# Moving accumulators between PSUM banks, loads into spare buffers, and the last norms in pairs, in a two-layer graph-attention kernel

## The chip, the cores and the metric

The kernel runs on one core of a Trainium2 chip. The metric is the device time of one execution in microseconds. The core has five engines that run their own instruction streams and meet at semaphores: TensorE (PE, matrix products; its weight loads are shown apart as PEld), VectorE (DVE), ScalarE (ACT), GpSimd (POOL) and SyncE (SP), which here only issues loads and stores. Matrix products land in PSUM, which has eight banks; a tile of 128 partitions by 512 float32 values fills one bank.

## The reference

There are 4096 nodes with 512 features, and one dense 0/1 adjacency matrix `adj` (4096 x 4096, symmetric, with ones on the diagonal). Two layers follow each other, each with a residual and a normalisation over the 512 features.

```python
def layer0(X, A, W, a_self, a_neigh, b):          # 8 heads of 64
    feats = einsum('nf,hfo->hno', X, W)
    dense = (feats . a_self)[:, :, None] + (feats . a_neigh)[:, None, :]
    dense = where(dense > 0, dense, 0.2 * dense) * A
    out = einsum('hij,hjo->hio', softmax(dense, -1), feats) + b
    return relu(out as (4096, 512))

def layer1(x, b, edge, ptr, Wq, bq, Wk, bk, Wv, bv):   # 32 graphs of 128 nodes
    mask = same graph
    a = where(mask, (x Wq' + bq) (x Wk' + bk)' / sqrt(512), 0)
    scores = (a + b + edge) * where(mask, 1, -1e6)
    return (softmax(scores) * mask) @ (x Wv' + bv)

x = layernorm(x + layer0(x, adj, ...))
x = layernorm(x + layer1(x, adj, adj, ...))
```

Layer 0 is a sum over all 4096 neighbours of each node. In layer 1 only the diagonal blocks of 128 by 128 count.

## The kernel before

**Layer 0.** The scores of a head depend on a node and on its neighbour only through one number each, so that the exponential of a score is the larger of two products. The kernel uses that: for a tile of 128 neighbours and 1024 nodes, one DVE instruction makes `q = max(p_row, d) * at` (L1560), with `p_row` a row of numbers of the nodes, `d` a column of the neighbours and `at` the adjacency tile. PE then adds three kinds of sums over the neighbours:

- `accf` (L1584): features `f_s` times `at`, two matmuls of weights for each tile and half;
- `acc` (L1607): features `g_s` times `q`, eight matmuls of 32 columns for each tile;
- `dens` (L1623): columns of exponentials `e_b` times `mark`, where `mark` tells which of the two products was larger (L1570 on ACT, one of eight at L1565 on DVE). In pass 0 there is also `ae` (L1499).

The work goes in four passes `r` over pairs of heads, each in four chunks `c` of 1024 nodes, each over 32 neighbour tiles `j`. A cycle takes eight `j` in passes 0 to 2 (`wide=8`), four in pass 3. PE's order in a cycle is: accf, then half of the bringing of later adjacency tiles, acc, dens, ae, and the other half of the bringing. In pass 0 bringing means eight transposes on PE (L614, `turned_steps`) into a PSUM bank, two casts on ACT (L625, `cast_steps`) into two `at` tiles, and a store of each to `at_d`; later passes load `at` from there. Some tiles are "folded": they take another formula (L1548, L1551, L1555), and their sums go to accf alone.

A setup makes the features of all nodes first. Its last part overlaps the first cycle: the transposes L773 give the last rows of exponentials, and `columns_of_last` turns them back into columns: four transposes L791 into a bank of `misc`, and the copy L794 into `pu_all`. `misc` deals out single PSUM banks in turn, for everything that is read back soon.

**PSUM.** The setup holds `ps_setup` (three banks) and `ps_feat` (four banks, the features). When they close, `ps_acc_f` takes five banks (`dens` one, `acc` two, `accf` two) from the place where ps_setup began, and the next pool takes the `ae` bank and, in pass 0, a second bank for `misc`. After pass 0, `misc` turns over three banks. A pool that takes the place of a closed one waits for the closed one's last readers.

**Layer 1** runs in blocks of four row tiles (512 nodes), interleaved with pass 3, in pieces that are dealt out by plan strings (`run_plan`); the last blocks run after pass 3. For each block, `rows_of_layer_0` loads the input `x1b` (L1257) and the heads of layer 0 from memory into `hp_l` (L1259, 384 columns, two buffers), adds them with a relu (L1264, the last 128 columns from `hst`, a tile in the chip's memory) and normalises them (`layernorm`: sums at L517 and L518 on DVE, the power on POOL at L520 and L521, the scaling at L525 on DVE, returned as a function that the plan calls at "F"). `layer_1` transposes them (L1085), forms the scores (L1105, L1132), and for each row tile the values (L1180, the bias L1189 into `v_t`, two buffers) and the outputs (L1196, L1198, a second `layernorm`, and the store L1206). In the last block the values of the last row tile are split: three of four matmuls before the outputs of the third, and the fourth after.

**What sets the order.** PE's instructions stand in program order. On the other engines a scheduler orders instructions as their inputs are due, except those that are pinned (`tc.keep_in_program_order`, `in_order`). SP's queue carries all loads in one line, so that a load that waits for its buffer holds the loads behind it.

Of the kernel before, what the change touches and what calls it, by code (L numbers as in the profile page):

```python
# [19 lines left out]
P = 128  # L20
# [384 lines left out]
def adjacency_streamed_path(  # L405
# [531 lines left out]
        columns_of_exponentials(NB - 1, misc([P, 4, 2 * H]))  # L937

    ckp = ctx.enter_context(tc.tile_pool(name="ck", bufs=2))
    psa = ctx.enter_context(tc.tile_pool(name="ps_acc_f", bufs=1, space=PSUM))  # L940
    dens = psa.tile([P, HB], F32, name="dens")
    nc.vector.memset(dens, 0.0)
# [62 lines left out]
    L1 = {}  # L1005
# [73 lines left out]
    def layer_1(blk, x1b, lp, lp1, lp2):  # L1079

        x1T = lp2.tile([P, FC, 4 * P], F32, name="x1T")
        for u in range(4):
            pt = misc([P, FC, P])
            for c in range(FC):
                nc.tensor.transpose(pt[:, c, :], x1b[:, u, ts(c, P)], ident)  # L1085
            nc.scalar.copy(x1T[:, :, ts(u, P)], pt)  # L1086
            if u == 1:
                yield
        a4 = lp.tile([P, 4, P], F32, name="a4")
        nc.sync.dma_start(  # L1090
            a4,
            bass.AP(
                tensor=adj.tensor,
                offset=adj.offset + 4 * blk * P * (N + 1),
                ap=[[N, P], [P * (N + 1), 4], [1, P]],
            ),
        )
        off = small.tile([P, 4], F32, name="off")
        rr = small.tile([P, 4], F32, name="rr")
        yield  # L1100
        zT = lp1.tile([P, FC, 4 * P], F32, name="zT")
        for c in range(FC):
            pz = misc([P, 4 * P])
            for f in range(FC):
                nc.tensor.matmul(  # L1105
                    pz,
                    L1["M"][:, f, ts(c, P)],
                    x1T[:, f, :],
                    start=(f == 0),
                    stop=(f == FC - 1),  # L1110
                )
            nc.scalar.activation(zT[:, c, :], pz, AF.Identity, bias=L1["zb"][:, c : c + 1])
            if c == 1:
                for u in range(4):
                    nc.scalar.activation(
                        a4[:, u, :], a4[:, u, :], AF.Copy, scale=2.0, accum_out=off[:, u : u + 1]
                    )
                    xu = lp.tile([P, F], F32, name="y_f")
                    nc.vector.tensor_tensor_reduce(
                        xu, x1b[:, u, :], L1["ub"], 1.0, 0.0, OP.mult, OP.add, rr[:, u : u + 1]  # L1120
                    )
                nc.gpsimd.tensor_scalar(off, off, 0.5, -float(P), op0=OP.mult, op1=OP.add)
                nc.gpsimd.tensor_add(off, off, n0[:, 4 * blk : 4 * blk + 4])
                nc.gpsimd.tensor_scalar(rr, rr, L1["cb"], None, op0=OP.add)
            if c % 2:
                yield
        pq = misc([P, 4, P])
        ns = a4
        nm = small.tile([P, 4], F32, name="nm_f")
        for u in range(4):  # L1130
            for f in range(FC):
                nc.tensor.matmul(  # L1132
                    pq[:, u, :],
                    zT[:, f, ts(u, P)],
                    x1T[:, f, ts(u, P)],
                    start=(u == 0 and f == 0),
                    stop=(f == FC - 1),
                    skip_group_check=True,
                )
        for u in range(4):  # L1140
            nc.vector.tensor_tensor_reduce(
                ns[:, u, :],
                pq[:, u, :],
                a4[:, u, :],
                -1.0,
                -LOWEST,
                OP.add,
                OP.min,
                nm[:, u : u + 1],
            )  # L1150
        nc.gpsimd.tensor_sub(nm, nm, rr)
        nc.gpsimd.tensor_scalar(nm, nm, 0.0, None, op0=OP.min)
        eb = small.tile([P, 4], F32, name="eb")
        nc.gpsimd.tensor_add(eb, nm, rr)
        den = small.tile([P, 4], F32, name="den_f")
        for u in range(4):
            nc.scalar.activation(
                ns[:, u, :],
                ns[:, u, :],
                AF.Exp,  # L1160
                bias=eb[:, u : u + 1],
                scale=-1.0,
                accum_out=den[:, u : u + 1],
            )
        e0 = small.tile([P, 4], F32, name="e0")
        nc.scalar.activation(e0, nm, AF.Exp)
        nc.gpsimd.tensor_tensor(e0, e0, off, OP.mult)
        nc.gpsimd.tensor_add(e0, e0, den)
        rd = small.tile([P, 4], F32, name="rd_f")
        nc.vector.reciprocal(rd, e0)  # L1170
        yield
        vs = {}

        def values(u, split=FC, pv=None):
            if pv is None:
                pv, fs = misc([P, F]), range(split)
            else:
                fs = range(split, FC)
            for f in fs:
                nc.tensor.matmul(  # L1180
                    pv,
                    x1T[:, f, ts(u, P)],
                    L1["wvT"][:, f, :],
                    start=(f == 0),
                    stop=(f == FC - 1),
                )
            if fs[-1] == FC - 1:
                vs[u] = lp.tile([P, F], F32, name="v_t")
                nc.vector.tensor_add(vs[u], pv, L1["bv"])  # L1189
            return pv  # L1190

        def rows_out(us):
            ys = []
            for u in us:
                po = misc([P, F])
                nc.tensor.matmul(po, pT[:, u, :], vs[u], start=True, stop=True)  # L1196
                y = lp.tile([P, F], F32, name="y_f")
                nc.vector.scalar_tensor_tensor(  # L1198
                    y, po, rd[:, u : u + 1], x1b[:, u, :], op0=OP.mult, op1=OP.add
                )  # L1200
                ys.append(y)
            layernorm(ys)()
            for i, u in enumerate(us):

                queue = nc.sync if blk >= NT // 4 - 2 else nc.gpsimd
                queue.dma_start(out[ts(4 * blk + u, P), :], ys[i])  # L1206

        values(0)
        pp = misc([P, 4, P])
        for u in range(4):  # L1210
            nc.tensor.transpose(pp[:, u, :], ns[:, u, :], ident)  # L1211
        pT = a4
        nc.scalar.copy(pT, pp)
        values(1)
        yield
        rows_out((0, 1))
        yield
        values(2)
        if blk == NT // 4 - 1:
            last = values(3, 3)  # L1220
            rows_out((2,))
            values(3, 3, last)
            yield
            rows_out((3,))
        else:
            values(3)
            yield
            rows_out((2, 3))
        yield
# [23 lines left out]
    def rows_of_layer_0(blk, hst, lp):  # L1253
        x1b = lp.tile([P, 4, F], F32, name="x1b")
        for u in range(4):
            it = 4 * blk + u
            nc.sync.dma_start(x1b[:, u, :], x[ts(it, P), :])  # L1257
            hp = lp.tile([P, F - FP], F32, name="hp_l")
            nc.sync.dma_start(hp, hs_d[ts(it, P), :])  # L1259
            for dst, src in (  # L1260
                (x1b[:, u, : F - FP], hp),
                (x1b[:, u, F - FP :], hst[:, it % CT, :]),
            ):
                nc.vector.scalar_tensor_tensor(dst, src, 0.0, dst, op0=OP.max, op1=OP.add)  # L1264
        plan["F"] = layernorm([x1b[:, u, :] for u in range(4)])
        return x1b

    def sums_to_rows(r, c, acc, accf, ae, u_row, later_by):
# [178 lines left out]
    def main_pass(r, ae=None, wide=4):  # L1447
# [9 lines left out]
        for c in range(NCH):  # L1457
# [46 lines left out]
                            stop=(j >= NT - 2),  # L1504
                        )

            acc = psa.tile([P, 2, HB], F32, name="acc")
            accf = psa.tile([P, 2, HB], F32, name="accf")
            marks = {}
            for j0 in range(0, NT, wide):  # L1510
# [70 lines left out]
                for j in cycle:  # L1581
                    for w in range(0 if folded(j) else 2):
                        for s in range(2):
# [4 lines left out]
                                start=(j == 0 and w == 0),  # L1588
                                stop=(j == NT - 1 and w == 1),
                            )  # L1590
                if at_step == 0:
                    columns_of_last()
                if r == 0 and (c, j0 + wide) == (NCH - 1, NT):

                    sums_over_a(c, cycle)
# [6 lines left out]
                for j in cycle:  # L1602
                    dst = accf if folded(j) else acc
                    for s in range(2):
                        for o in range(0, FP, 32):
# [6 lines left out]
                                stop=(j == NT - 1),  # L1612
                                skip_group_check=folded(j),
                            )
                if r == 0:
                    pieces(c, j0 // 4, 1)

# [36 lines left out]
    with tc.tile_pool(name="ps_ae", bufs=1, space=PSUM) as psx:  # L1654
        ae = psx.tile([P, HB], F32, name="ae")
        nc.vector.memset(ae, 0.0)
        banks.append(psx)
        main_pass(0, ae, wide=8)
        banks.remove(psx)
    first_pass.close()  # L1660
    banks.extend([ctx.enter_context(tc.tile_pool(name="ps_misc2", bufs=2, space=PSUM))] * 2)
    with tc.tile_pool(name="wl1", bufs=1, side="right") as wp:
        pools["wl1"] = wp
        work.append(weights_of_layer_1(keep, wp))
# [70 lines left out]
```

## Time and profile before

| what | us |
|---|---|
| median of three runs (2026.96 to 2030.07) | 2030.03 |
| the profiled execution | 2029.65 |
| its span | 2027.9 |
| PE busy | 1999.2 (99% of the span) |
| DVE busy | 1756.0 (87%) |
| ACT busy | 1524.7 (75%) |
| POOL busy | 231.2 (11%) |

The mean clock that PE was granted is 0.996 of full speed. The 40 slices of the span show PE at nine tenths or more in all but the last, which has seven tenths.

In the views below, a line of the timeline gives the start in us, the time from the first to the last of the merged instructions, the engine, the line of the code, the operation with the tile that it writes and those that it reads, the size, and how many were merged; in brackets stands the idle time of the engine before it and what ended that. A line of the waits gives who waited for whom, the total, the number of waits and the longest.

### The profile page before, as it was taken

The numbers are of one execution on the slowest core, as the hardware profiler recorded it, in microseconds if no ns is written. First come the engines' busy times: TensorE is split into PE (matmuls) and PEld (weight loads), VectorE is DVE, ScalarE is ACT, GpSimd is POOL, SyncE is SP. The second block draws the span as 40 slices with busy tenths as digits, with TensorE's granted clock in tenths as the row PEclk, the third lists the DMA queues.
The fourth block names the chain that finished last, engine by engine and source line by source line (L and its number), as shares of the span: only waits on it lengthen the run. The fifth ranks groups of instructions, "written<-read, shape, count | busy, mean of one in ns | idle before, by whom it ended". The sixth has DMA issues, their size and how long they took to land. (4 is left out here: it accounts for less than half of the span.)

```text
span 2027.9 us, 38096 instructions
## 1 busy us (share of the span) xinstructions
PE 1999.2 (99%) x14961; PEld 1023.0 (50%) x14961; DVE 1756.0 (87%) x2212; ACT 1524.7 (75%) x1872; POOL 231.2 (11%) x362
## 2 busy tenths in 40 slices
PE   9999999999999999999999999999999999999997
PEld 8884454545444444445445444444444444445443
DVE  5668999999999999898999999999997897899754
ACT  3348888888879898889889899999786666567420
POOL 1222222222200000000000000000020210211111
PEclk9999999999999999999999999999999999999998
DMA  6999999999999999799999899989976775775211
GB/s 210 248 328 270 296 283 277 287 292 295 323 368 342 364 343 327 257 340 310 317 318 333 304 347 334 333 280 366 320 255 197 243 246 163 233 278 161 73 55 44
DMA packets 209673, 555.74 MB, mean 274 GB/s; under 512 B 25068, under 2 KB 66412, under 8 KB 209484
## 3 DMA queue, kind: packets, MB, share of 16 engines
q1 hardware_dynamic: 145132, 430.64, 60.9%
q0 software_dynamic: 62272, 122.04, 23.4%
q8 instruction: 120, 1.97, 0.4%
q10 hardware_dynamic: 2080, 0.52, 0.1%
q14 instruction: 69, 0.57, 0.1%
HBM read 496.11 MB, written 107.35 MB: 298 GB/s over the span
## 5 line engine op out<-in xcount | busy, mean ns | idle before, releaser
L1560 DVE SCALAR_TENSOR_TENSOR q<-p_row,d_all,at 128x1024 f32<-128x1024 f32 x952 | 1154.9, 1277 | 94.2 <-PE acc L1607 38.4
L1570 ACT ACTIVATE mark<-q,nb_all 128x1024 fp8e4<-128x1024 f32 x824 | 907.6, 1148 | 137.9 <-DVE q L1560 126.9
L1607 PE MATMUL acc<-q,g_s 128*32 128x512 f32 x7616 | 841.9, 593 | 1.2 <-DVE q L1560 0.4
L1607 PEld LDWEIGHTS acc<-q,g_s 128*32 128x32 f32 x7616 | 248.5, 110 | 556.3 <-issue 495.5
L1584 PE MATMUL accf<-at,f_s 128*128 128x512 f32 x1904 | 464.3, 399 | 2.8 <-ACT at L625 2.7
L1584 PEld LDWEIGHTS accf<-at,f_s 128*128 128x128 f32 x1904 | 351.4, 189 | 109.2 <-issue 26.3
L1248 ACT ACTIVATE ck<-ck,neg_half_f 128x1024 f32<-128x1024 f32 x128 | 146.0, 1140 | 26.0 <-DMA ck<-in_adj_dram 25.7
L1249 ACT ACTIVATE ck<-ck,neg_quarter 128x1024 f32<-128x1024 f32 x128 | 146.4, 1144 | 1.9
L1555 ACT ACTIVATE mark<-q,below 128x1024 fp8e4<-128x1024 f32 x72 | 81.6, 1145 | 78.4 <-DVE q L1551 77.9
L1623 PE MATMUL dens<-mark,e_b 128*6 128x512 fp8e4 x2048 | 125.9, 379 | 1.8 <-DVE mark L1565 1.6
L807 PE MATMUL ps_fe<-w_sb_f,xT_f 128*128 128x264 f32 (+1 forms) x512 | 121.7, 395 | 1.0 <-ACT xT_f L727 1.0
L625 ACT CAST at<-ps_m 128x1024 fp32r<-128x1024 fp8e4 x124 | 117.2, 1026 | 0.0
L1180 PE MATMUL ps_m<-wvT,x1T 128*128 128x512 f32 x256 | 114.4, 594 | 0.0
L1105 PE MATMUL ps_m<-x1T,M_sb 128*128 128x512 f32 x256 | 113.0, 595 | 0.3 <-ACT x1T L1086 0.3
L807 PEld LDWEIGHTS ps_fe<-w_sb_f,xT_f 128*128 128x128 f32 x512 | 100.6, 200 | 15.7 <-ACT xT_f L727 1.8
L1371 POOL DMA_DIRECT2D hs_d<-hst x12 | 10.7, 896 | 827.6 <-DVE hst L1361 814.5
L626 POOL DMA_DIRECT2D at_d<-at x128 | 71.0, 555 | 269.9 <-ACT at L625 141.8
L1565 DVE TENSOR_SCALAR mark<-q,d_all 128x1024 fp8e4<-128x1024 f32 x128 | 95.9, 749 | 5.0 <-PE accf L1584 0.5
L1623 PEld LDWEIGHTS <-e_b 128*6 128x6 bf16 x2048 | 55.8, 86 | 79.3 <-issue 37.1
L1551 DVE SCALAR_TENSOR_TENSOR q<-q,c_all,at 128x1024 f32<-128x1024 f32 x72 | 90.5, 1274 | 0.0
L1105 PEld LDWEIGHTS ps_m<-x1T,M_sb 128*128 128x128 f32 x256 | 47.9, 190 | 59.6 <-issue 57.8
L1180 PEld LDWEIGHTS ps_m<-wvT,x1T 128*128 128x128 f32 x256 | 47.6, 190 | 56.4 <-issue 55.2
(209 smaller groups left out, 1315.3 us busy)
## 6 DMA issues: line engine op xcount, KB each, us to landing
at<-at_d SPq DMA_DIRECT2D x384, 512.0 KB, 6.0
at_d<-at POOLq DMA_DIRECT2D x128, 512.0 KB, 17.4
ck<-in_adj_dram SPq DMA_DIRECT2D x128, 512.0 KB, 5.5
f_s<-f_d SPq DMA_DIRECT2D x107, 512.0 KB, 7.5
g_s<-g_d SPq DMA_DIRECT2D x128, 256.0 KB, 5.8
f_d<-fst POOLq DMA_DIRECT2D x16, 1024.0 KB, 7.9
a_b<-in_adj_dram POOLq DMA_DIRECT2D x32, 512.0 KB, 21.1
p_row<-pu_d SPq DMA_DIRECT2D x32, 512.0 KB, 6.7
```

Source lines behind the costliest of these rows:

```text
L625: ends_of_setup["ACT"] = nc.scalar.copy(at, both[:, :, k])
L807: nc.tensor.matmul(pf[:, q, :, cols], tile_j(xTs[k][:, c].rearrange("p u n -> p (u n)"), u), w_sb[:, c, 4 * q : 4 * q + 4, cols], start=(c ...
L1105: nc.tensor.matmul(pz, L1["M"][:, f, ts(c, P)], x1T[:, f, :], start=(f == 0), stop=(f == FC - 1),)
L1180: nc.tensor.matmul(pv, x1T[:, f, ts(u, P)], L1["wvT"][:, f, :], start=(f == 0), stop=(f == FC - 1),)
L1248: tc.keep_in_program_order(nc.scalar.activation(ck, ck, AF.Square, bias=neg_half))
L1249: nc.scalar.activation(ck, ck, AF.Abs, bias=neg_quarter, accum_out=binp[:, k : k + 1])
L1560: ends_of_setup["Q"] = nc.vector.scalar_tensor_tensor(q, p_row[h], d_j, ats[r, c, j].bitcast(F32), op0=OP.max, op1=OP.mult)
L1565: nc.vector.tensor_scalar(mark, q, d_j, None, op0=OP.is_gt, saturate=False)
L1570: nc.scalar.activation(mark, q, AF.Sigmoid, bias=nb_all[:, j, hh : hh + 1], scale=BIG, saturate=False,)
L1584: nc.tensor.matmul(accf[:, s, :], f_s[j // 4][:, j % 4, w, :], ats[r, c, j][:, ts(s, HB)], start=(j == 0 and w == 0), stop=(j == NT - 1 an ...
L1607: nc.tensor.matmul(dst[o : o + 32, s, :], g_s[j // 4][:, j % 4, h, o % FH : o % FH + 32], qs[j, h][:, ts(s, HB)], start=(j == 0), stop=(j ...
L1623: nc.tensor.matmul(dens[lo : lo + 6, :], e_b[:, j, 2 * r + h, :], marks[j, h][:, ts(s, HB)], start=(j == 0), stop=(j == NT - 1),)
```

## The change

- **PSUM pools.** `acc` gets a pool of its own (`ps_acc_q`, two banks) and the second bank of `misc` another (`ps_misc1`); these two open first and so take the three banks of the setup. `ps_acc_f` keeps `dens` and `accf`, and with the `ae` bank it takes the four banks of the features. After pass 0 `misc` gets one more bank, where it got two.
- **The last exponentials' columns.** `columns_of_last()` is called after the acc matmuls of the first cycle, where it was called after the accf matmuls.
- **Spare buffers.** For the third and fourth row tile of a block, the heads of layer 0 are loaded into a `v_t` buffer, where all four went through the two `hp_l` buffers.
- **The last norms.** In the last block the four rows of layer 0 are normalised as two pairs, each with its own power on POOL.
- **The last row tiles.** The outputs of the third row tile are called ahead of the last matmul of the fourth's values, the addition that ends those values is pinned, and the normalisation of the third comes after it.

```diff
@@ setup, end
     ckp = ctx.enter_context(tc.tile_pool(name="ck", bufs=2))
+    psq = ctx.enter_context(tc.tile_pool(name="ps_acc_q", bufs=1, space=PSUM))
+    banks.append(ctx.enter_context(tc.tile_pool(name="ps_misc1", bufs=1, space=PSUM)))
     psa = ctx.enter_context(tc.tile_pool(name="ps_acc_f", bufs=1, space=PSUM))
     dens = psa.tile([P, HB], F32, name="dens")
     nc.vector.memset(dens, 0.0)
@@ layer_1
-        def values(u, split=FC, pv=None):
+        def values(u, split=FC, pv=None, pinned=False):
...
                 vs[u] = lp.tile([P, F], F32, name="v_t")
-                nc.vector.tensor_add(vs[u], pv, L1["bv"])
+                in_order(pinned, nc.vector.tensor_add(vs[u], pv, L1["bv"]))
             return pv
-        def rows_out(us):
-            ys = []
+        ys = {}
+
+        def outputs(us):
             for u in us:
                 po = misc([P, F])
                 nc.tensor.matmul(po, pT[:, u, :], vs[u], start=True, stop=True)
-                y = lp.tile([P, F], F32, name="y_f")
+                y = ys[u] = lp.tile([P, F], F32, name="y_f")
                 nc.vector.scalar_tensor_tensor(
                     y, po, rd[:, u : u + 1], x1b[:, u, :], op0=OP.mult, op1=OP.add
                 )
-                ys.append(y)
-            layernorm(ys)()
-            for i, u in enumerate(us):
+
+        def rows_out(us):
+            outputs([u for u in us if u not in ys])
+            layernorm([ys[u] for u in us])()
+            for u in us:
...
-                queue.dma_start(out[ts(4 * blk + u, P), :], ys[i])
+                queue.dma_start(out[ts(4 * blk + u, P), :], ys[u])
...
             last = values(3, 3)
+            outputs((2,))
+            values(3, 3, last, True)
             rows_out((2,))
-            values(3, 3, last)
@@ rows_of_layer_0
-            hp = lp.tile([P, F - FP], F32, name="hp_l")
+            hp = lp.tile([P, F - FP if u < 2 else F], F32, name="hp_l" if u < 2 else "v_t")
+            hp = hp[:, : F - FP]
             nc.sync.dma_start(hp, hs_d[ts(it, P), :])
...
-        plan["F"] = layernorm([x1b[:, u, :] for u in range(4)])
+        n = 2 if blk == NT // 4 - 1 else 4
+        ends = [layernorm([x1b[:, u + v, :] for v in range(n)]) for u in range(0, 4, n)]
+
+        def finish(pinned=False):
+            for end in ends:
+                end(pinned)
+
+        plan["F"] = finish
@@ main_pass
-            acc = psa.tile([P, 2, HB], F32, name="acc")
+            acc = psq.tile([P, 2, HB], F32, name="acc")
             accf = psa.tile([P, 2, HB], F32, name="accf")
...
-                if at_step == 0:
-                    columns_of_last()
                 if r == 0 and (c, j0 + wide) == (NCH - 1, NT):
...
                                 skip_group_check=folded(j),
                             )
+                if at_step == 0:
+                    columns_of_last()
                 if r == 0:
                     pieces(c, j0 // 4, 1)
@@ around the passes
         ae = psx.tile([P, HB], F32, name="ae")
         nc.vector.memset(ae, 0.0)
-        banks.append(psx)
         main_pass(0, ae, wide=8)
-        banks.remove(psx)
     first_pass.close()
-    banks.extend([ctx.enter_context(tc.tile_pool(name="ps_misc2", bufs=2, space=PSUM))] * 2)
+    banks.append(ctx.enter_context(tc.tile_pool(name="ps_misc2", bufs=1, space=PSUM)))
```

## The prediction

> Lines are numbered as in the kernel before. All times are of the one profiled execution (2029.65 us, span 2027.9 us, so 1.75 us lie around the span).
>
> **What bounds the kernel.** I read the busy line of the page first, then what TensorE (PE) waits for, then the stretches around its longest waits.
>
> ```profile
> PE 1999.2 (99%) x14961; PEld 1023.0 (50%) x14961; DVE 1756.0 (87%) x2212; ACT 1524.7 (75%) x1872; POOL 231.2 (11%) x362
> ```
>
> PE is taken in 99% of the span, so only 2027.9 - 1999.2 = 28.7 us are idle. [...] The waits of PE speak for the row:
>
> ```profile
> PE accf L1584 <- ACT at L625: 2.7, 4, 2.1
> PE ps_m L1085 <- DVE x1b L525: 1.8, 1, 1.8
> PE ps_m L614 <- DVE pu_all L794: 1.6, 1, 1.6
> PE dens L1623 <- DVE mark L1565: 1.6, 1, 1.6
> ```
>
> (Total us, times, longest.) If another engine set the pace, it would stop PE in every cycle. Instead these are single waits, and none is on a load in the main passes. I take it that a wait of PE shortens the span one for one, unless something behind it cannot follow. The change touches four waits, in three places.
>
> **Place 1, the first cycle of pass 0.** PE's instructions in order of time:
>
> ```profile
> 153.73 0.60 PE L773 MATMUL ps_set<-ident_f,pu_j 128*24 128x128 f32 x4
> 156.42 9.21 PE L1584 MATMUL accf<-at,f_s 128*128 128x512 f32 x32 [2.10 <-ACT at L625]
> 168.16 0.61 PE L614 MATMUL ps_m<-ident_b,a_b 128*128 128x128 bf16 x8 [1.63 <-DVE pu_all L794]
> 168.70 13.94 PE L1607 MATMUL acc<-q,g_s 128*32 128x512 f32 x128
> 186.08 6.80 PE L1584 MATMUL accf<-at,f_s 128*128 128x512 f32 x28
> ```
>
> (a) `accf` and `dens` lay on the setup banks, whose last reader is the cast L625 that ends at 156.37. On the features' banks the last reader is L741, done at 153.04, so accf follows L773 at 154.33: -2.10. The cast still feeds the sixth tile of the cycle, which accf reaches 5 x 0.97 = 4.9 us after its start, at 159.2.
>
> (b) The four transposes L791 (0.35 us of PE) and the copy L794 behind them leave the place between accf and acc. The copy was at 167.89 on VectorE (DVE), behind eight q and a mark, and the second L614 waited for its bank: -1.63. The four transposes are only moved past acc's 128 matmuls, net 0. The copy goes behind 16 q, to about 178 to 181 by the order of DVE's instructions; the L614 that then waits for its bank comes at about 181. Its values serve only later tiles. What is late next there: at most 0.3 us.
>
> (c) The clock. Two stretches with a wait of PE at their start (columns: stretch, PE, PEld, DVE, ACT, POOL, granted clock, DMA share, GB/s):
>
> ```profile
> 156.50:160.00 3.50, 3.50 (x9) 2.79 (x10) 3.45 (x5) 3.47 (x4) 3.34 (x5) 0.52 0.72 261
> 1953.00:1956.20 3.20, 1.43 (x6) 0.40 (x5) 1.95 (x7) 0.69 (x1) 1.92 (x3) 1.00 0.00 0
> ```
>
> Right after the 2.10 us wait the granted clock is 0.52 for about 3.5 us; the wait of 1.77 us at 1954 left it at 1.00. The price: accf's 32 matmuls took 9.21 us, at the rate of the second cycle (28 in 6.80 us) 7.77, so 1.44 us. [...] I follow the row: -1.44, ends 0 and -1.44.
>
> Sum for PE: 2.10 + 1.63 + 1.44 = 5.17. Can the others follow?
>
> - DVE: the first q moves ahead of L865, to 155.35; the other seven still follow it at 157.54, so eight q end near 166.0 instead of 167.2. The 2.62 us in which DVE then waited for acc to free a q go: acc starts at 154.33 + 7.77 + 2 x 0.54 = 163.2. Eight more q (9.66 us) after the mark (0.67) end at 176.3, 4.1 us earlier. acc needs the last at 163.2 + 15/16 x 13.94 = 176.3: no margin, but no loss.
> - ScalarE (ACT): busy from 153.5 through the table load, marks and casts to 170.86; its only idle there is 1.18 us, so the marks of the second half end at 179.2 instead of 180.4. dens runs from about 177.6 to 179.5 and needs the last of them at 179.4: up to 0.2 us.
> - Second cycle: its last four casts (187.86 now) stand behind a mark fed by DVE's chain, which moves by 4.1 - 0.2 (the copy) = 3.9 us; accf has 1.2 us of slack there (tile 12 cast at 188.8, used at 189.97). Allowed shift about 5.0.
> - DMA: the adjacency tiles land at 173.36 and 183.5, used at 185.2 and 192.7; f_s (issued 176.23, landed 183.95) is released by acc and moves with it.
>
> So of 5.17 I keep 4.5, with ends 1.5 (the clock dips anyway and half of the rest is lost behind DVE or ACT) and 5.2. The memsets of dens and ae (0.48 each) are only reordered on DVE, which idles 1.76 us there now.
>
> **Place 2, rows in pass 3 (1658).** Loads hp_l for the third and fourth row tile wait in SyncE's queue until DVE has used the first two:
>
> ```profile
> 1656.70 0.56 DVE L1264 SCALAR_TENSOR_TENSOR x1b<-hp_l,x1b 128x384 f32<-128x384 f32 x1 [3.82 <-DMA hp_l<-hs_d]
> 1657.97 0.38 PE L1623 MATMUL dens<-mark,e_b 128*6 128x512 fp8e4 x3 [1.62 <-DVE mark L1565]
> ```
>
> The load was issued at 1649.23; the mark that PE needed stood behind it. After, these loads go to spare v_t buffers, wait for PE's L1196 of the block before, and leave at about 1635, ahead of f_s and x1b in the queue. The two additions (0.47 us each) then run before two q: those end 0.94 later, at 1653.8, where acc needs the second at 1653.9. The mark ends at 1654.5, needed at 1656.3. Gain 1.62 less 0.1: 1.5, ends 0 and 1.62. The same is done in all blocks; elsewhere PE did not wait, so 0.
>
> SyncE pays nothing for it but 2 x 0.45 us of issue per block: the x1b loads behind already wait for L1198, which follows L1196. Loads delayed by it land well ahead: the f_s issued at 1638.95 landed at 1644.32 for use at 1664.9; the smallest margin for PE that I found from the landings is 13 us (1834.6 for 1847.6).
>
> **Place 3, the last norms (1956).**
>
> ```profile
> 1949.31 0.56 DVE L1264 SCALAR_TENSOR_TENSOR x1b<-hp_l,x1b 128x384 f32<-128x384 f32 x1 [1.30 <-DMA hp_l<-hs_d]
> 1953.67 0.58 POOL L520 TENSOR_SCALAR rstd_f<-mv_f 128x4 f32<-128x4 f32 x1 [6.86 <-DVE mv_f L518]
> 1954.33 1.04 POOL L521 TENSOR_TENSOR rstd_f<-rstd_f,neg_half 128x4 f32<-128x4 f32 x1
> 1955.41 1.92 DVE L525 TENSOR_SCALAR x1b<-x1b,mv_f,rstd_f 128x512 f32<-128x512 f32 x4 [1.25 <-POOL rstd_f L521]
> 1956.11 1.99 PE L1085 MATMUL ps_m<-ident_f,x1b 128*128 128x128 f32 x16 [1.77 <-DVE x1b L525]
> ```
>
> The 1.30 us go with the early loads (-1.3). In pairs, POOL handles two rows while DVE sums the other two; two wide it took 0.22 + 0.73 us (1942.84, 1943.14), so the second pair costs about 0.7 less: the first row is normalised near 1953.5, the fourth at 1954.9. PE is free at 1954.34 and takes 0.5 us per row: 1.77 gone, 0.8 to spare. Two more instructions on POOL (0.95 us) delay nothing. From 1956 to 2012 PE has no gap, so it is kept: 1.8, ends 0.5 and 1.8.
>
> **The last row tiles** change nothing: the addition L1189 stays behind the row sums L517 in DVE's order, and PE's 1.31 us wait for it at 2014.9 stays. That part does not do what it says: 0.
>
> **Sum.** 4.5 + 1.5 + 1.8 = 7.8 us: 2029.65 - 7.8 = 2021.85. The median shown (2030.03) is 0.4 above the profiled execution, so 2022.2.
>
> **Rivals.**
>
> 1. Only part arrives (same): the clock dips anyway and DVE and ACT swallow half of the rest in pass 0 (1.5), and the two q at 1653 push the stall on to acc (0). 1.5 + 1.8 = 3.3: 2026.7. For it: DVE is busy 37.7 of 40 us from 200 to 240, and the margins of 0 to 0.2 us above. Against: DVE and ACT had 2.62 and 1.18 us idle in the first cycle.
> 2. One place fails (still faster): without place 3, 2024.0; without the clock, 2023.6; without place 2, 2023.7.
> 3. Slower: a v_t load at the head of SyncE's queue waits for PE and holds the at and f_s loads behind it, for the five blocks that run beside pass 3. It decides from a hold of 13 us on; each us beyond it stops PE once per block. To end 0.2% slower it must eat the gain and 4 more, 11.9 us, or 2.4 us in each of the five: 2034. Against: the condition is met before that of the x1b loads behind it, which costs nothing now.
>
> **Chances.** 0.2% (4 us) is about what a measurement of this kernel tells from no change. My forecast 0.52, rival 2 0.16, rival 1 0.19, rival 3 0.13: faster 0.68, same 0.19, slower 0.13. The forecast's own range is 2021 to 2024; the whole range reaches up through rival 1 to 2028.5 and down to 2020.8 (all ends full, 8.6, and half a us of scatter).
>
> **What would show it.** accf starts at 154.4 and takes 7.8 us; PE has no wait for L794; the granted clock after 156.5 is 1.0; PE's second cycle starts near 181.5; no wait of dens near 1650; no PE wait for L525; the 1.3 us wait for L1189 still there. Wrong would be: accf at 154.4 but still 9 us, new waits of accf on L625 in the second cycle, or PE waits on f_s or at in pass 3.

## The result and the profile after

The changed kernel takes 2021.45 us (median of 6 runs, 2020.72 to 2022.70) beside 2030.05 us for the kernel before (6 runs, 2026.96 to 2034.23); the ratio is 0.9951, with a 95% interval of 0.9942 to 0.9961. A second set of runs on another occasion gave 2023.59 beside 2030.74 and a ratio of 0.9962 (0.9949 to 0.9976). So it is faster: by 8.6 and 7.2 us between the medians, and by 9.9 us (7.9 to 11.8) and 7.7 us (4.9 to 10.4) by the two ratios, which are not the plain quotients of the medians. The forecast was 7.8 us and 2022.2 us. The median of 2021.45 lies in the forecast's range of 2020.8 to 2028.5; the first ratio times the median shown (0.9951 x 2030.03) is 2020.1, which is 0.7 us below its low end.

What PE waits for in the changed kernel (total us, times, longest; its lines stand up to 14 further down than those of the kernel before):

```profile
PE ps_m L1199 <- DVE v_t L1191: 1.3, 1, 1.3
...
PE accf L1598 <- ACT at L625: 0.7, 3, 0.3
...
PE ps_m L1087 <- DVE x1b L525: 0.5, 1, 0.5
```

Of the four waits that the change touched, three are gone (accf's 2.1, those for the copy and for the mark), and the fourth is 0.5 instead of 1.8. The wait for L1191 at the end is the one that was to stay.

The first cycle, PE's and DVE's instructions in order of time, and then the stretch in which the clock was at half before (its columns: stretch, PE, PEld, DVE, ACT, POOL, granted clock, DMA share, GB/s):

```profile
154.07 7.56 PE L1598 MATMUL accf<-at,f_s 128*128 128x512 f32 x32
...
162.48 15.83 PE L1619 MATMUL acc<-q,g_s 128*32 128x512 f32 x128
...
182.20 6.91 PE L1598 MATMUL accf<-at,f_s 128*128 128x512 f32 x28
```

```profile
166.69 9.65 DVE L1574 SCALAR_TENSOR_TENSOR q<-p_row,d_all,at 128x1024 f32<-128x1024 f32 x8
```

The end of acc, in a view that begins at 176.3:

```profile
176.40 1.91 PE L1619 MATMUL acc<-q,g_s 128*32 128x512 f32 x12
```

The stretch of the half clock:

```profile
156.50:160.00 3.50, 3.50 (x17) 2.91 (x16) 3.08 (x4) 3.47 (x4) 3.33 (x5) 1.00 0.72 260
```

accf starts 2.35 us earlier and runs at the full clock, 7.56 us instead of 9.21. acc starts 6.2 us earlier, but takes 15.8 us instead of 13.9, since it waits for DVE's q: the last one is done at 176.34, and the last 12 of acc's 128 records start at 176.40. The granted clock is 1.00 all the while. The second cycle starts 3.88 us earlier.

Pass 3 at the place where dens waited, and the last block (PE, then DVE and POOL):

```profile
1649.93 2.26 PE L1637 MATMUL dens<-mark,e_b 128*6 128x512 fp8e4 x30
1652.12 7.13 PE L1107 MATMUL ps_m<-x1T,M_sb 128*128 128x512 f32 x16
```

```profile
1948.05 1.99 PE L1087 MATMUL ps_m<-ident_f,x1b 128*128 128x128 f32 x16 [0.46 <-DVE x1b L525]
```

```profile
1939.02 0.56 DVE L1271 SCALAR_TENSOR_TENSOR x1b<-hp_l,x1b 128x384 f32<-128x384 f32 x1 [0.88 <-DMA x1b<-in_x_dram]
1940.86 0.56 DVE L1271 SCALAR_TENSOR_TENSOR x1b<-hp_l,x1b 128x384 f32<-128x384 f32 x1 [0.32 <-DMA x1b<-in_x_dram]
```

dens has no gap any more. In the last block the 1.30 us for hp_l are gone, and 1.20 us of waits for x1b have come.

**Where the time went, in seven traces.** I matched PE's groups of instructions between each trace and the trace of before and took the difference of their starts. Each row rests on one execution. The table gives how this difference grows over a stretch (us; minus is gained), by the times of the trace of before. Two traces of the changed kernel are shown.

| kernel | setup, to 150 | first cycle, to 182 | to 1350 | pass 3, to 1900 | last block, to 1957 | to 2014 |
|---|---|---|---|---|---|---|
| changed | 0.0 | -3.9 | +0.2 | -3.1 | -1.3 | 0.0 |
| changed, second trace | +2.2 | -3.9 | +0.6 | -3.7 | -0.7 | 0.0 |
| pools alone | +1.4 | +0.4 | +0.1 | -0.6 | +0.1 | 0.0 |
| columns alone | +1.2 | -1.8 | +0.4 | 0.0 | +1.4 | +0.5 |
| spare buffers alone | +0.4 | 0.0 | +0.5 | -3.7 | -0.7 | 0.0 |
| changed, no spare buffers | -1.4 | -3.9 | +1.0 | +2.3 | -1.1 | 0.0 |
| changed, no pairs | -1.8 | -3.9 | +4.1 | -3.8 | 0.0 | 0.0 |

The setup, which the change doesn't touch, differs by up to 4 us between executions, and the clock differs with it. From 28 to 32 and from 32 to 36 us the granted clock is 0.77 and 0.80 in the trace of before, and 0.83 and 0.75 in the first trace of the changed kernel, whose setup ends at the same time. It is 0.58 and 0.57 in the pools alone, 1.4 us later, and 0.73 and 0.50 in the second trace of the changed kernel, 2.2 us later. The profile has PE busy for the whole of these stretches in all four, so what makes the clock fall in the setup stays open. A wait of PE for xT_f near 17 us (L807; 1.0 us before, 0.9 and 1.7 us in the two traces of the changed kernel, 2.0 us in two waits in the pools alone) also differs between the traces and takes part in the spread. Between the two traces of the changed kernel the setup makes 2.2 of the 3.0 us; how much of the spread of all runs it makes is not shown.

### The profile page after: what moved, and what is told of

Read it like the earlier page. It is cut to its first block, busy times and chain, and to the rows that moved or that the text cites. A ratio compares the mean times of both kernels' runs of the same rounds, so it can differ in the third digit from the quotient of the medians.

```text
span 2019.4 us, 38098 instructions
## 1 busy us (share of the span) xinstructions
PE 1998.2 (99%) x14961; PEld 1023.9 (51%) x14961; DVE 1755.8 (87%) x2212; ACT 1522.7 (75%) x1872; POOL 231.0 (11%) x364
## 3 DMA queue, kind: packets, MB, share of 16 engines
q8 instruction: 120, 1.97, 0.4%
## 4 chain that ended last, share of the span: by engine, by line
PE 83%; DVE 11%; issue 2%; ACT 2%; DMA 1%; SPq 0%; POOL 0%; DVEq 0%; POOLq 0%; ACTq 0%
PE acc L1619 33%; PE accf L1598 20%; DVE q L1574 6%; PE ps_fe L807 5%; PE ps_m L1182 5%; PE ps_m L1107 5%; PE dens L1637 4%; PE accf L1619 3%; DVE q L1565 1%; PE ps_m L1134 1%; DVE q L1562 1%; PE ps_m L1199 1%; ACT at L625 1%; PE ps_m L614 1%; PE ps_m L1087 1%
## 5 line engine op out<-in xcount | busy, mean ns | idle before, releaser
L807 PE MATMUL ps_fe<-w_sb_f,xT_f 128*128 128x264 f32 (+1 forms) x512 | 122.0, 395 | 0.9 <-ACT xT_f L727 0.9
L625 ACT CAST at<-ps_m 128x1024 fp32r<-128x1024 fp8e4 x124 | 117.3, 1027 | 0.0
L807 PEld LDWEIGHTS ps_fe<-w_sb_f,xT_f 128*128 128x128 f32 x512 | 100.8, 201 | 15.6 <-ACT xT_f L727 1.6
```

Source lines behind the costliest of these rows:

```text
L625: ends_of_setup["ACT"] = nc.scalar.copy(at, both[:, :, k])
L807: nc.tensor.matmul(pf[:, q, :, cols], tile_j(xTs[k][:, c].rearrange("p u n -> p (u n)"), u), w_sb[:, c, 4 * q : 4 * q + 4, cols], start=(c ...
```

## The experiments

**The pools alone.**

```diff
+    psq = ctx.enter_context(tc.tile_pool(name="ps_acc_q", bufs=1, space=PSUM))
+    banks.append(ctx.enter_context(tc.tile_pool(name="ps_misc1", bufs=1, space=PSUM)))
...
-            acc = psa.tile([P, 2, HB], F32, name="acc")
+            acc = psq.tile([P, 2, HB], F32, name="acc")
```

> The kernel before with the new PSUM pools alone (acc on the setup's banks, accf, dens and ae on the features'); columns, buffers and norms as before. Theory (the two edits at the start work only together): accf starts at 154.1 and takes 7.6 us at full clock, but the copy L794 still stands behind eight q and a mark on DVE, at 166.7, so the second L614 waits for it about 4.5 us (162.4 to 166.9), acc starts near 167.4 and the second cycle's accf only 1.2 us earlier than before (184.9). Total about 2028.8. Rival (each edit gives its own wait): -2.1 and -1.4 arrive in full, second cycle 3.5 us earlier (182.6), total about 2026.5.

The ratio is 1.0004 (0.9995 to 1.0013), so nothing is gained. PE, then a stretch with its clock (this trace runs 1.4 us late from the setup):

```profile
155.48 7.56 PE L1586 MATMUL accf<-at,f_s 128*128 128x512 f32 x32
...
168.37 0.86 PE L614 MATMUL ps_m<-ident_b,a_b 128*128 128x128 bf16 x8 [4.42 <-DVE pu_all L794]
169.16 15.32 PE L1609 MATMUL acc<-q,g_s 128*32 128x512 f32 x128
```

```profile
168.30:172.00 3.70, 3.63 (x24) 1.39 (x27) 0.01 (x1) 3.22 (x4) 2.50 (x4) 0.54 1.19 159
```

The wait of 4.4 us for the copy came as expected. What I had not expected is that the half clock came behind it (0.54 from 168.3 to 172), and cost acc 1.4 us (15.32 instead of 13.94): the second cycle is 0.4 us later than before, not 1.2 earlier.

**The columns alone.**

```diff
-                if at_step == 0:
-                    columns_of_last()
                 if r == 0 and (c, j0 + wide) == (NCH - 1, NT):
...
+                if at_step == 0:
+                    columns_of_last()
```

> The kernel before with columns_of_last moved behind acc alone. Theory: accf still waits 2.1 us and runs at half clock for 3.5 us; acc starts 2.0 us earlier (166.7), is PE's own 13.9 us long or ends 1.9 us after the last q (178.4 + 1.9), so near 180.6, and after the four transposes dens is 1.4 us earlier than before (181.0), accf of the second cycle at 184.7. Total about 2028.6. Rival (it is worth nothing alone, since DVE's q bind anyway): second cycle within 0.3 us of before, 2030. With the run of the pools alone: if both singles add up to the 3.9 us that both together gave, the parts are independent; I expect 2.6.

The ratio is 0.9997 (0.9988 to 1.0007). The first cycle gained 1.8 us, near the 1.4 expected. The trace loses it again in the last block, where PE waited 2.1 us for L525 instead of 1.8 and the clock fell to half behind that wait (0.50 from 1956.95 to 1960.3):

```profile
1956.27 3.08 PE L1085 MATMUL ps_m<-ident_f,x1b 128*128 128x128 f32 x16 [2.10 <-DVE x1b L525]
```

```profile
1956.95:1960.30 3.35, 3.35 (x18) 3.35 (x17) 3.16 (x13) 2.33 (x4) 0.09 (x1) 0.50 0.00 0
```

The pools lose 0.4 us, the columns gain 1.8, and both together gain 3.9: the parts are not independent. One removes a wait in front of accf, the other the wait that grows in its place (4.42 us for the copy in the pools alone, 1.63 before).

**Work for PE in the idle time.** Two kernels. The first puts eight matmuls into the bank that `misc` deals next, the second into the one that is free; nobody reads the result.

```diff
+                if at_step == 0:
+                    fill = banks[-1].tile([P, HB], F32, name="ps_m")
+                    for _ in range(8):
+                        nc.tensor.matmul(
+                            fill, f_s[0][:, 0, 0, :], ats[r, c, 0][:, :HB], start=True, stop=True
+                        )
                 for j in cycle:
                     for w in range(0 if folded(j) else 2):
```

(The first has `fill = misc([P, HB])`.)

> The kernel before with eight matmuls more (128 x 512, about 1.9 us, into a free misc bank that nobody reads) between L773 and accf in the first cycle, in the place of the idle 2.1 us. All else is kept, so accf still starts when the cast L625 is done. Theory (the half clock follows the idle time): granted clock 1.0 from 156.5 to 160, accf takes 7.6 to 7.8 us instead of 9.2; the time saved is lost again to the copy L794, for which the second L614 then waits 3.1 us instead of 1.6, so the total stays at 2030. Rival (the half clock comes from the light work before 154 or from a window of its own): the clock is about 0.5 there again and accf takes about 9.2 us.

The ratio is 1.0007 (0.9999 to 1.0015). This one missed: the bank that `misc` dealt was still read by a cast, so the eight matmuls waited too, and PE idled 3.51 us instead of 2.10. Both the filling (3.78 us for eight, where they took 2.09 us in the second kernel) and the start of accf ran at a lower clock (0.50 from 156.5 to 160 and 0.85 from 160 to 164), so this run decides nothing between theory and rival.

> The kernel before with eight matmuls more in the idle time before accf, this time into the bank that is already free at 154.3 (their result isn't read). Theory (a stretch of half clock follows when PE idles about 2 us or more with little work just before): they run from 154.4 to 156.4 at 0.24 us each, the clock stays at 1.0 from 156.5 to 160 and accf takes 7.6 us. The second L614 then idles about 3 us for the copy L794, and the half clock comes after that instead, so acc takes 15.3 us instead of 13.9: nothing gained, about 1.4 us later at dens than before. Rival (the half clock is tied to this place, not to idle time): clock about 0.5 from 156.5 to 160 and accf 9.2 us as before.

The ratio is 1.0008 (0.9999 to 1.0017). PE, and two stretches:

```profile
155.16 2.09 PE L1584 MATMUL ps_m<-at,f_s 128*128 128x512 f32 x8
157.50 7.58 PE L1590 MATMUL accf<-at,f_s 128*128 128x512 f32 x32 [0.25 <-ACT at L625]
...
169.24 1.01 PE L614 MATMUL ps_m<-ident_b,a_b 128*128 128x128 bf16 x8 [3.26 <-DVE pu_all L794]
```

```profile
156.50:160.00 3.50, 3.25 (x15) 2.36 (x14) 2.38 (x4) 3.48 (x5) 2.79 (x5) 1.00 0.77 297
...
168.00:172.00 4.00, 2.76 (x20) 1.25 (x23) 1.15 (x3) 3.82 (x5) 2.13 (x4) 0.57 1.19 172
```

With the idle time filled, the clock stays at 1.00 from 156.5 to 160 and accf takes 7.58 us; around the end of the next idle time (3.26 us) it is 0.57. So the half clock here went with PE's idle time and not with the place. The price was larger than I expected: the second cycle came 3.0 us later, not 1.4, since acc started 0.4 us later (1.1 us of the setup taken out), and its first 116 records took 15.21 us, where 116 of the 128 make 12.6 of the 13.94 us before.

**The changed kernel without the spare buffers, and the spare buffers alone.**

```diff
-            hp = lp.tile([P, F - FP if u < 2 else F], F32, name="hp_l" if u < 2 else "v_t")
-            hp = hp[:, : F - FP]
+            hp = lp.tile([P, F - FP], F32, name="hp_l")
```

> The changed kernel with all four row tiles' heads loaded through the two hp_l buffers again (norms in pairs and the rest kept). Theory: the wait of dens for the mark comes back (1.6 to 1.7 us), the small waits in pass 3 outside the two places come back (0.9 us by 1640, 0.6 us by 1950), and in the last block the pairs alone still save about 1 us, since the first pair is scaled while POOL works on the second. So it is 3.3 us slower than the changed kernel: about 2024.8, a shift of 5.0 against before. Rival (the small gains of pass 3 are those of the start, or scatter): 1.7 us slower, about 2023.2. Second rival (the early loads made all of the last norms' gain): 4.5 us slower, 2026.

> The kernel before with the spare v_t buffers for the third and fourth row tile alone. Theory (the loads through two hp_l buffers stop PE at different blocks in each execution, not only at the one place of the profile of before): PE gains about 3.5 us between 1350 and 1900 against the mean of the profiles with two buffers, and little in the last block, where the same loads delay x1b; median about 3.8 us below before, and less scatter than before (whose standard deviation is 2.1 us). Rival (the profile of before showed the whole price): 1.7 us at 1658 and nothing elsewhere, about 2029.5, with the scatter of before.

Without the buffers the changed kernel takes 2026.71 us (ratio 0.998, 0.9973 to 0.9987). The buffers alone give 2026.18 us (0.9976, 0.9967 to 0.9985), with a standard deviation of 0.9 us over 12 runs. The buffers are worth more than my reading of one profile said: alone 4.9 us by the ratio, and between 3.6 and 5.9 us in the changed kernel, whose ratio was 0.9951 or 0.9962. By the traces they gain 3.1 to 3.8 us from 1350 to 1900, and without them the kernel with the early start loses another 2.3 there. In that trace the same stall stands at another block than in the trace of before, where PE had no wait at this place (DVE, then PE):

```profile
1819.22 0.56 DVE L1270 SCALAR_TENSOR_TENSOR x1b<-hp_l,x1b 128x384 f32<-128x384 f32 x1 [3.37 <-DMA hp_l<-hs_d]
```

```profile
1820.50 0.39 PE L1636 MATMUL dens<-mark,e_b 128*6 128x512 fp8e4 x3 [1.17 <-DVE mark L1578]
```

So the rivals that count 1.7 us for the buffers fall: the profile of before did not show the whole price. The second rival of the run without buffers came near in its total (4.5 us slower than the changed kernel), but not in its cause, since the last block still gained 1.1 us.

The stall also moves without an early start: in the trace of the columns alone, where PE enters pass 3 within 0.2 us of before, dens doesn't wait near 1658 and waits 0.84 us at 1822, behind a wait of DVE for hp_l of 3.04 us. Whether the early start adds to it, as the 2.3 us suggest, is not shown.

**One norm of four rows in the last block.**

```diff
-        n = 2 if blk == NT // 4 - 1 else 4
+        n = 4
```

> The changed kernel with one norm of four rows in the last block again. Theory: with the early loads the last sum is there at 1945.6, POOL takes 0.6 + 1.0 us as it does for the second pair, and the scaling starts within 0.2 us of where it does now, since in DVE's order it stands behind the four L1121 in both: 0 to 0.3 us slower than the changed kernel. Rival (the pairs make the gain of the last norms): the wait of L1087 for L525 is 1.3 to 1.8 us again, 0.8 to 1.3 us slower.

The median is 2022.67 us (ratio 0.9958, 0.9942 to 0.9973; four runs), which can't be told from the changed kernel. The trace tells more. POOL, DVE and PE:

```profile
1948.06 0.58 POOL L520 TENSOR_SCALAR rstd_f<-mv_f 128x4 f32<-128x4 f32 x1 [6.35 <-DVE mv_f L518]
1948.73 1.34 POOL L521 TENSOR_TENSOR rstd_f<-rstd_f,neg_half 128x4 f32<-128x4 f32 x1
```

```profile
1950.10 1.91 DVE L525 TENSOR_SCALAR x1b<-x1b,mv_f,rstd_f 128x512 f32<-128x512 f32 x4 [0.32 <-POOL rstd_f L521]
```

```profile
1950.80 1.99 PE L1087 MATMUL ps_m<-ident_f,x1b 128*128 128x128 f32 x16 [1.77 <-DVE x1b L525]
```

The whole wait of 1.77 us is back, as the rival said, but most of the difference isn't made by the missing pairs. DVE waited 2.05 us for x1b here, and 1.20 and 1.71 us in the two traces of the changed kernel, so that its sums came later. For the power of four (1.34 us) DVE waited only 0.32 us, since L525 stands behind the four L1121 in its order with pairs or without, as my theory had it. So in this trace the missing pairs cost about 0.3 us, and the rest of the longer wait (1.3 and 0.7 us longer than in those two traces) goes with the later x1b. Where the heads come late, the pairs are worth more: in the changed kernel without the buffers L525 doesn't wait for POOL at all, where it waited 1.25 us in the kernel before, and PE's wait is 0.45 us. The last block gained 0.0 without pairs, 0.7 and 1.3 with both, 0.7 by the buffers alone and 1.1 by the pairs without the buffers.

The same trace shows a wait that no trace of the kernel before has, in pass 0:

```profile
474.06 1.11 PE L614 MATMUL ps_m<-ident_b,a_b 128*128 128x128 bf16 x16 [2.13 <-DMA a_b<-in_adj_dram]
475.10 15.54 PE L1619 MATMUL acc<-q,g_s 128*32 128x512 f32 x128
```

```profile
474.00:478.00 4.00, 3.94 (x32) 1.68 (x36) 0.00 (x0) 3.99 (x5) 1.20 (x3) 0.62 1.05 384
```

An adjacency tile landed after PE had come to it, the clock was 0.62 from 474 to 478, behind the idle time of 2.13 us, and 4.1 us were lost, more than the first cycle had gained. (These tiles are loaded on POOL's queue, at L602, and not on SP's.) PE came to it at 471.93 (474.06 less the wait) and at 477.23 in the trace of before. There the same tile landed at 476.56, 24.5 us after its issue and 0.7 us before PE's transposes, so little was to spare. Of six traces with the early start, two lost 2.6 and 4.1 us between 182 and 1350 (0.8 of the 2.6 in the second cycle, by another edit, below) and the others 0.2 to 1.0; the five others lost at most 0.6 against the trace of before. That the early start causes these late tiles is likely from this, but not shown.

**Two tries at a better kernel.** The first gives the two marks that DVE makes in the first cycle to ACT and pins the row sums of the third of the last row tiles behind L1191.

```diff
-                        if j % 4 == 3 and h == 1:
+                        if j % 4 == 3 and h == 1 and at_step:
...
-            nc.vector.bn_stats(stats[:, u, :], src)
+            ins = nc.vector.bn_stats(stats[:, u, :], src)
+            if pinned:
+                tc.keep_in_program_order(ins)
...
-            layernorm([ys[u] for u in us])()
+            layernorm([ys[u] for u in us], us == (2,))()
```

> The changed kernel with two edits: in the first cycle the two marks of DVE (L1579) go to ACT, and the row sums L517 of the third of the last row tiles are pinned, so that they follow the addition L1191 of the fourth's values. Theory (acc of the first cycle now ends two matmul groups after DVE's last q): without the mark the last eight q end 0.67 us earlier, acc ends 0.6 us earlier, and about 0.5 is left at the second cycle; the last addition comes 0.6 us earlier and with it PE's last wait (1.3 to 0.7) and the end. Together 1.1 us faster than the changed kernel, about 2020.3. Rival (ACT's marks or casts are the bound in the first cycle): the second cycle starts no earlier, 0.6 us in all.

The median is 2023.29 us (ratio 0.9966, 0.9952 to 0.9979), so no gain over the changed kernel is seen. The first cycle came 0.8 us earlier, as it should if DVE's q are the bound there, and the second cycle gave it all back, since ACT's casts were later (accf's waits for L625 are 1.3 us in all instead of 0.7). The pin brought its 0.5 us: PE's last wait is 0.8.

The second keeps the pin, leaves the marks, and sends the v_t and a4 loads of the last block behind the four x1b loads.

```diff
+            if u == 0:
+                for v in range(4):
+                    ins = nc.sync.dma_start(x1b[:, v, :], x[ts(4 * blk + v, P), :])
+                    ends_of_setup["X"] = ins
...
-            nc.sync.dma_start(hp, hs_d[ts(it, P), :])
+            with following(blk == NT // 4 - 1 and u >= 2, "X"):
+                nc.sync.dma_start(hp, hs_d[ts(it, P), :])
```

The same stands around the load of a4. The first part of the edit puts the four x1b loads ahead in all blocks; pass 3 gained 3.8 us in its trace, as in others.

> The changed kernel with two edits near the end: in the last block the four x1b loads go out ahead of the two v_t loads and of the a4 load, where they stood behind them; and the row sums L517 of the third of the last row tiles are pinned behind the addition L1191. Theory (in the last block the wait for x1b has taken the place of the wait for hp_l, because six loads now share the transfer engines ahead of it): DVE's waits for x1b of 0.9 + 0.3 us go, the wait of L1087 for L525 (0.5 us in the changed kernel) goes, and PE's last wait is 0.8 instead of 1.3: 1.0 us faster than the changed kernel. Rival (x1b lands late because of its own four loads): only the 0.5 us at the end.

> The changed kernel as it is, for its scatter and beside the run before it. Theory: median within 1 us of 2021.5, standard deviation about 1 us against 2 us before. In single executions a load of an adjacency tile in pass 0 may stop PE by up to 4 us, as in the profile of the run without pairs, since the earlier start has used up its margin: then the median is up to 2023 and the scatter as large as before.

The kernel with x1b first takes 2020.66 us (ratio 0.9949, 0.9936 to 0.9963), beside 2023.59 for the changed kernel in the same set (0.9962, 0.9949 to 0.9976). With five runs each the intervals overlap, so the difference is not shown by the times. The traces show the part that is sure: no wait for L525 at all, 1.8 us gained in the last block against 0.7 of the run beside it, and 0.5 at the end, so 1.6 us (1.0 against the first trace of the changed kernel). DVE's first use of x1b in the two (the kernel with x1b first, then the changed one):

```profile
1939.83 0.55 DVE L1278 SCALAR_TENSOR_TENSOR x1b<-hp_l,x1b 128x384 f32<-128x384 f32 x1
```

```profile
1941.32 0.56 DVE L1271 SCALAR_TENSOR_TENSOR x1b<-hp_l,x1b 128x384 f32<-128x384 f32 x1 [1.16 <-DMA x1b<-in_x_dram]
```

The loads were issued at 1936.84 and 1937.10, so 3.0 and 4.2 us before. This kernel has the lowest median of all. The changed kernel came out above both forecasts of its expectation here (within 1 us of 2021.5, or up to 2023), with a standard deviation of 1.3 us (2.1 for before in the same set). Its trace shows no stop of 4 us for an adjacency tile, only one of 0.2, but the late setup of the table.

## Why the prediction was right and where it was wrong

**The step that failed is the zero in place 2:** "The same is done in all blocks; elsewhere PE did not wait, so 0." It took the worth of the spare buffers from one wait in one execution. In the runs the buffers gave 3.1 to 3.8 us in pass 3 where 1.5 was forecast, and alone they shortened the whole kernel by 4.9 us (3.0 to 6.7) by the ratio. The waits for hp_l had the mechanism that the prediction gave them; it is the size of this term that was wrong. With it the low end of the range failed: "half a us of scatter" was too little for a kernel whose three runs shown spread over 3.1 us, and six runs over 7.3.

**PE as the bound: right in the main.** At the four waits and in the slow stretch behind the first, 8.3 us went, and about 6.9 us of that arrived (3.9 + 1.7 + 1.3).

**(a) The banks: right,** 2.35 against 2.10. **(b) The columns: right,** no wait is left, and the L614 behind the copy did not wait.

**(c) The clock: right to follow the row.** The stretch of half clock went with the wait, 1.65 us against 1.44 (accf 7.56, not 7.77). No run shows the 0 at the other end of this term, a slow stretch that stays without the wait: where accf doesn't wait, in the changed kernel and in the pools alone, the clock is 1.00 from 156.5 to 160 and accf takes 7.56 us, and with the idle time filled it is 1.00 and 7.58 us. In other places a lower clock came with other idle times of PE: 0.54 (168.3 to 172) with 4.42 us in the pools alone, 0.57 (168 to 172) with 3.26 us in the second kernel with eight matmuls more, 0.62 (474 to 478) with 2.13 us without the pairs, and 0.50 (1956.95 to 1960.3) with 2.10 us in the columns alone. With the 1.77 us at 1954 in the trace of before it stayed at 1.00 (1953 to 1959). So some waits cost more than their own length here: behind the 4.42 us, acc took 1.4 us longer. Which idle times bring the clock down, and why it also fell in the setup with PE busy, no run here shows.

**Can the others follow: the step on DVE failed.** "acc needs the last at 163.2 + 15/16 x 13.94 = 176.3: no margin, but no loss" takes one q for each sixteenth of acc. acc works by tiles, and within each half of a tile through both heads, so only 4 of a tile's 16 records can go before its second q, and 12 of the 128 stand behind the last one. By the prediction's own times acc needed it at 163.2 + 116/128 x 13.94 = 175.8, half a us before it was there. In the trace it was done at 176.34, as forecast, and acc ended 1.97 us later, at 178.31. The first cycle gave 3.9, not 4.5. **The step on DMA was read in too few places:** I checked the tiles of the first cycles, and the tile that came late was one near 470.

**Place 2: right at its one place** (1.7 against 1.5). The other blocks, put at 0, gave 1.4 us in the first trace of the changed kernel and about 2 in the second, and the kernel with the early start and without the buffers lost 2.3 more than before. The profile of before was one execution; DVE's waits for hp_l stood at six places in it (13.3 us in all), and which of them reach PE changes.

**Place 3: half right.** "The 1.30 us go with the early loads" failed: v_t and a4 went out just ahead of x1b, x1b landed 3.9 to 5.7 us after its issue instead of 2.9 to 4.1, and DVE waited 1.20 us for it. With x1b first, PE's wait for L525 is gone. "SyncE pays nothing for it but 2 x 0.45 us of issue" counted the queue and not the transfers. "Two wide it took 0.22 + 0.73 us, so the second pair costs about 0.7 less" failed too: beside DVE's L1121 the second pair took 0.57 + 1.01. The pairs were worth about 0.3 us beside the buffers, where L1121 holds L525 back in any case. The last block gave 1.3 and 0.7 us instead of 1.8.

**The last row tiles: right,** the wait stays at 1.3 us; pinning the row sums brings 0.5.

**The sum.** By the first trace 3.9 - 0.2 + 3.1 + 1.3 and 0.4 at the last store make 8.5 (8.4 between the two profiled executions), against 4.5 + 1.5 + 1.8 = 7.8: the start and the last block were put too high, and the spare buffers at less than half of their worth. That the sum came within 1 us is in part luck, since these errors offset each other. The first ratio makes 9.9 us; its last 1.5 us lie within its interval and no trace assigns them. Rival 1 came true only in part (DVE did bind in the first cycle); rival 3 did not: no trace shows PE waiting for f_s or at in pass 3.

## What to carry to other kernels

A load that waits for its buffer can stall the engine that uses it at other places in each execution: here DVE waited for hp_l six to eight times in each of six traces with the two buffers (13.2 to 16.3 us in all), and dens stood still behind such a wait near 1658 in one trace (1.62 us) and at 1820 in another (1.17 us). Count every such wait of that engine, not only those that reach the bound in one profile. Two waits in a row on the bound engine may have to go together: here removing the first alone left the second cycle 0.4 us later, since the second wait grew from 1.63 to 4.42 us and a clock of 0.54 came behind it. When a load is moved earlier, look at what lands next to it (here x1b, 3.9 to 5.7 us after its issue instead of 2.9 to 4.1), not only at what is issued behind it.

## What the runs showed of the hardware

- PE's granted clock around PE's idle times: 0.52 (156.5 to 160) with 2.10 us in the kernel before; 0.73 and 0.81 (156.5 to 160, 160 to 164) with 2.09 us and 0.50 (1956.95 to 1960.3) with 2.10 us in the columns alone; 0.54 (168.3 to 172) with 4.42 us in the pools alone; 0.50 (156.5 to 160) with 3.51 us in the first and 0.57 (168 to 172) with 3.26 us in the second kernel with eight matmuls more; 0.62 (474 to 478) with 2.13 us without the pairs. It was 1.00 with 1.77 us in the kernel before (1953 to 1959), and with the eight matmuls in the place of the idle time (156.5 to 160).
- In the setup the clock from 28 to 32 and from 32 to 36 us, with PE shown busy all the while, was 0.77 and 0.80 before, 0.83 and 0.75 and then 0.73 and 0.50 in the two traces of the changed kernel, and 0.58 and 0.57 in the pools alone.
- In the last block the four x1b loads landed 3.9 to 5.7 us after their issue in the changed kernel, with two v_t loads and an a4 load just ahead of them, and 2.9 to 4.1 us in the kernel before, with the a4 load alone. With those loads just behind them, DVE used the first x1b 3.0 us after its issue without a wait, and waited 0.40 us for a later one (1942.37).
- In the changed kernel POOL's L520 and L521 on 128 x 2 took 0.22 and 0.72 us while DVE made row sums (1944.39 and 1944.69), and 0.57 and 1.01 us beside DVE's custom operation L1121 (1945.72 and 1946.38). The power of four rows took 1.04 us with DVE idle (1954.33 before) and 1.34 us beside L1121 (1948.73 without pairs).
